# The third layer's entry and its second pass: first strips and bases on ScalarE's DMA queue, tables in pieces, later needs issued later, memory tracked by tiles

## The chip, the cores and the metric

The kernel runs on one core of a Trainium2 chip, in fp32. The metric is the device time of one execution in microseconds; the time of a kernel is the median of its runs.

## The reference, cut to what matters

The kernel applies four residual layers to an image batch `x` of shape (8, 56, 56, 192), each to the group-normalized `x` (32 groups of channels):

```
x = x + L0(gn(x))     # gated Toeplitz (decaying FFT convolution) along both axes
x = x + L1(gn(x))     # outlook attention, 3x3 neighbourhoods
x = x + L2(gn(x))     # gated attention in 8x8 windows, with a linear part over all windows
x = x + L3(gn(x))     # scans along rows, columns and diagonals
```

The change concerns the third layer, L2, cut here:

```
uvb = silu(xw @ W_uv + b_uv)                # xw: windows of 64 tokens, 192 channels
u, v, base = uvb[:384], uvb[384:768], uvb[768:]          # base: 128 wide
qq, qk = rope in the window of (base * gq_g + gq_b), (base * gk_g + gk_b)
lq, lk = rope in the image of (base * lq_g + lq_b), (base * lk_g + lk_b)
attn = square(relu(qq @ qk.T / 64 + rel_bias[REL_INDEX]))
kv   = sum over all windows of an image of lk.T @ v      # 128 x 384
out  = u * (attn @ v + lq @ kv) @ W_proj + b_proj
```

`kv` is needed as a whole before any output, so the layer makes two passes over the image.

## The kernel before, in words

The layers run one after the other in one program and keep x in DRAM between them. Images are worked on in pairs (`NPAIR` is 4): 128 of an image's 192 channels lie on the partitions of one tile, and the other 64 of both images share a second tile. In layer 1 and in the second pass of the third layer the instruction order on TensorE, VectorE (DVE), ScalarE (ACT) and GpSimd (POOL) is the order in which the source writes it (`manual_schedule`); in the first pass of the third layer that holds for TensorE alone, and the other engines' order, like that of the DMAs on SyncE (SP), is set by a planner when the program is built. Every engine then works through its queue in order, and a DMA is issued from the queue of the engine that the source names. A DMA or an instruction waits until the tiles that it writes are free and those that it reads are filled; between pools that follow each other in the same memory this is tracked by pool or, with `reuse_waits="tile"`, by tile.

**Group norms.** `GroupNormPairs` (L1135 on) holds a matrix `gmat` (576 KB) that spreads group sums over channels by tiny matmuls (L1153). The statistics of a pair are gathered strip by strip with `bn_stats` (L1007 in layer 1). At a pair's end three steps follow: `means`, `deviations` and `tell`. `deviations` and `tell` each use one burst of matmuls, `tell` also a square root on ACT (L1182) and four small DMAs that write the scales and shifts to DRAM as `norm`. In layer 1 these steps are put off into the next units as a list `late`; what remains in the list after the last unit is run at once, at the layer's end.

**Third layer, entry.** `layer2` (L1236) builds its own `GroupNormPairs` and the `Takeover` (L1194), which loads what the fourth layer needs (`am`, `vec`, `res`). Then SP fetches the norms of all four pairs (16 DMAs, L1262 and L1263). ACT's queue issues the weights of pass 2 (`wub`, `bub`, `wpr`, `bpr`, `gbs`) and four rotation tables, of which `cos_img` and `sin_img` have 1568 KB each. SP loads `ident`, the weights and bias of pass 1 (`wvb`, `bvb`) and the cos rows; ACT's queue loads the sin rows (1600 KB each). From these DVE and POOL make the key tables `tn`, `ta` and `tb`, 128 x 3200 each, in five operations (L1355 to L1359). Then the first two strips of x are fetched (`load`, L1276 to L1278: six DMAs per strip), the first is normalized (`wa`, `wb`, L1301, or L49 for the part that DVE takes), and SP issues 64 DMAs that lay out the relative bias row by row (L1466).

**Third layer, pass 1.** `groups` lists for each pair 13 groups of up to two chunks of 128 tokens of both images, 52 in all. In loop step n, group n is projected to v and base (`project`, PE `v` L1390), biased on DVE (`sm`, L1400) and passed through silu on ACT (`vb`, L1401); v is stored to DRAM (L1412) and base is turned into keys with the tables (`keys`: POOL L1419, L1420, DVE L1424, L1427). For group n-2, base is transposed and stored (`turn`, PE `t` L1436, ACT `bt` L1440) and the keys are summed with v (`sum_up`, PE `kv` L1450). `vb` has four buffers, the PSUM tile `v` three, the PSUM tile `t` one. A strip covers seven chunks, so a pair has four strips; `fetch` runs two strips ahead.

**Third layer, pass 2.** `units` lists strips of 448 tokens, 28 in all. `fetch2` issues the loads of a unit: x, the base both straight (`bt`, L1509) and with its halves swapped (`bs`, L1512), and v (`vt`, L1515). `rotate` makes qq, qk and lq from them (ACT L1524 and L1525, POOL L1535, DVE L1538 and L1539). TensorE starts a unit with the window products (`b`, L1550).

## Time and profile before

| what | value |
|---|---|
| three runs | 4262.56, 4271.02, 4275.62 us; median 4271.02 |
| profiled execution | 4265.11 us, of which its span is 4263.3 |
| granted TensorE clock, mean | 0.971 |
| TensorE busy | 3954.9 us, 93% of the span |
| VectorE, ScalarE, GpSimd busy | 55%, 42%, 35% |
| layer 1's last y matmul (L978) ends | 2724.2 us from the span's start |
| first projection of the third layer (L1390) | 2775.45 us |
| kv sums of groups 0, 1 and 2 (L1450) | 2812.13, 2820.80, 2829.36 us |
| last kv sum ends | 3225.08 us |
| first window product of pass 2 (L1550) | 3244.86 us |

The profile is one execution; its instants count from the start of its span. "Waited for" is idle time of an engine in front of an instruction, put down to what came last. Figures of one stage are read from windows of the trace, not from the shares of the whole span.

### The profile page before, as it was taken

How to read it: one execution, taken by the hardware profiler on the slowest of the kernel's cores; microseconds unless marked ns; L12 is line 12 of the kernel's file. 1: busy time of each engine (PE TensorE's matmuls, PEld its weight loads, DVE VectorE, ACT ScalarE, POOL GpSimd, SP SyncE). 2: the span in 40 equal slices, each digit the busy share in tenths (PEclk: the TensorE clock that was granted, in tenths of full speed). 3: DMA queues.
4: the chain of work that ended last, by engine and by line, in shares of the span. 5: the costliest groups of instructions: out<-in, count | busy, mean ns of one | idle time of the engine just before them, and what ended most of it. 6: DMA issues, size and time to landing. Idle time of an engine off the chain costs nothing.

```text
span 4263.3 us, 106441 instructions
## 1 busy us (share of the span) xinstructions
PE 3954.9 (93%) x46380; PEld 2553.1 (60%) x46380; DVE 2345.1 (55%) x3396; ACT 1781.1 (42%) x2020; POOL 1512.6 (35%) x1294
## 2 busy tenths in 40 slices
PE   6989999999999999999699999679998999998997
PEld 3666656666665656666366666434444555555997
DVE  4536565554656555464534444266666666664664
ACT  2434444334444433443233334133334555554664
POOL 3222232223223221332233333143334444444776
PEclk9999999999999999999799999889999999999999
DMA  6755242332524233241324444555547676664243
GB/s 142 141 106 145 62 114 71 81 86 62 145 62 115 74 81 84 62 122 47 92 75 107 97 105 108 146 153 169 166 141 186 167 166 162 151 156 112 73 115 94
DMA packets 379606, 484.13 MB, mean 114 GB/s; under 512 B 175780, under 2 KB 324372, under 8 KB 377236
## 3 DMA queue, kind: packets, MB, share of 16 engines
q1 hardware_dynamic: 373636, 466.97, 43.0%
q10 hardware_dynamic: 5504, 10.35, 0.8%
q8 instruction: 365, 5.98, 0.6%
q14 instruction: 101, 0.83, 0.1%
HBM read 321.49 MB, written 155.65 MB: 112 GB/s over the span
## 4 chain that ended last, share of the span: by engine, by line
PE 73%; DVE 7%; issue 7%; DMA 4%; SPq 3%; POOL 3%; ACT 2%; DVEq 0%; POOLq 0%; ACTq 0%
PE c L294 9%; PE v L1390 6%; PE c L395 6%; PE h L1892 5%; PE c L301 5%; PE c L481 4%; PE c L436 4%; PE c L943 4%; PE c L461 3%; PE y L978 3%; PE kv L1450 3%; PE c L443 3%; PE c L486 2%; DVE ol L357 2%; PE c L949 2%
## 5 line engine op out<-in xcount | busy, mean ns | idle before, releaser
L325 POOL TENSOR_TENSOR qv<-s,s 128x392 f32<-128x392 f32 (+3 forms) x320 | 569.3, 1799 | 1424.6 <-ACT s L310 1354.2
L294 PE MATMUL c<-xa,wqv 128*128 128x392 f32 x1152 | 435.9, 520 | 7.7 <-ACT or L357 4.8
L310 ACT ACTIVATE s<-c,bqv 128x784 f32<-128x784 f32 (+1 forms) x320 | 278.2, 910 | 389.9 <-PE c L301 232.8
L319 DVE TENSOR_TENSOR qv<-s,s 128x784 f32<-128x784 f32 (+1 forms) x160 | 190.4, 1190 | 268.2 <-ACT s L310 268.1
L357 ACT COPY or<-c 56x1024 f32<-56x1024 f32 x224 | 225.6, 1007 | 256.3 <-DVE ol L357 240.9
L294 PEld LDWEIGHTS c<-xa,wqv 128*128 128x128 f32 x1152 | 212.2, 196 | 177.2 <-issue 44.2
L395 PEld LDWEIGHTS c<-or,ol 120*64 120x64 f32 x9216 | 277.8, 138 | 55.7 <-issue 47.4
L395 PE MATMUL c<-or,ol 120*64 120x56 f32 x9216 | 287.2, 223 | 18.5 <-DMA ol<-ed 9.0
L357 DVE COPY ol<-c 56x1024 f32<-56x1024 f32 x224 | 261.4, 1208 | 63.4 <-PE c L352 63.4
L450 ACT ACTIVATE s<-c,bp 128x448 f32<-128x448 f32 x224 | 129.7, 630 | 271.0 <-PE c L443 271.0
L1390 PE MATMUL v<-wvb,wa 128*128 128x512 f32 (+1 forms) x400 | 192.6, 614 | 50.0 <-ACT wa L1301 30.7
L301 PE MATMUL c<-xb,wqv 64*128 64x392 f32 x1152 | 233.6, 519 | 0.0
L1923 POOL TENSOR_TENSOR y<-y,s 128x448 f32<-128x448 f32 x168 | 185.1, 1102 | 90.1 <-ACT s L1902 90.1
L1892 PE MATMUL h<-ringv,am 128*64 128x57 f32 (+1 forms) x4400 | 191.8, 235 | 18.3 <-DVE ringv L1879 11.3
L481 PE MATMUL c<-po,wo 128*128 128x448 f32 x448 | 198.1, 564 | 10.8 <-DVE po L470 10.8
L436 PE MATMUL c<-xa,wp 128*128 128x224 f32 x896 | 192.0, 358 | 3.2 <-issue 3.2
L1892 PE MATMUL h<-ringh,am 128*64 128x57 f32 (+1 forms) x4400 | 185.9, 231 | 8.0 <-DVE ringh L1898 7.8
L1401 ACT ACTIVATE vb<-sm 128x1024 f32<-128x1024 f32 (+1 forms) x100 | 103.7, 1038 | 211.2 <-issue 187.2
L424 DVE TENSOR_TENSOR acca<-c,acca 128x392 f32<-128x392 f32 (+1 forms) x120 | 67.3, 586 | 222.0 <-PE c L486 204.8
L352 PE MATMUL c<-ident,qv 64*120 64x64 f32 x3584 | 144.3, 227 | 44.2 <-ACT or L357 38.3
L1892 PEld LDWEIGHTS h<-ringv,am 128*64 128x64 f32 x4400 | 167.2, 140 | 21.5 <-DVE ringv L1879 12.2
L943 PE MATMUL c<-wv,xc 128*126 128x192 f32 x896 | 175.4, 339 | 0.7 <-DVE s L903 0.6
(224 smaller groups left out, 7690.6 us busy)
## 6 DMA issues: line engine op xcount, KB each, us to landing
or<-tt SPq DMA_DIRECT2D x252, 196.0 KB
ol<-tt SPq DMA_DIRECT2D x252, 196.0 KB
vt<-v SPq DMA_DIRECT2D x56, 672.0 KB
v<-vb SPq DMA_DIRECT2D x96, 384.0 KB
x<-x SPq DMA_DIRECT2D x112, 168.0 KB
x<-x SPq DMA_DIRECT2D x112, 112.0 KB
bt<-bs SPq DMA_DIRECT2D x28, 448.0 KB
bs<-bs SPq DMA_DIRECT2D x56, 224.0 KB
```

Of the source, the lines that this page charges most:

```text
L294: nc.tensor.matmul(ps[:, h, 0:n], wqv[0][:, j, :], xn[0][:, at : at + n], start=True, stop=False,)
L301: nc.tensor.matmul(ps[:, h, 0:n], wqv[1][rows, j, :], xn[1][rows, g * n : (g + 1) * n], start=False, stop=True,)
L310: nc.scalar.activation(t, ps[rows, :, 0:n], AF.Silu, bias=bqv[rows, j : j + 1])
L319: nc.vector.tensor_tensor(sub(qv[rows, 7 * g :, 64 + H - 1 :], (HH * 120, 2), (120, 7), (-1, H)), *(t.rearrange("p u (h w) -> p u h w", w= ...
L325: eng.tensor_tensor(sub(qv[rows, w0:, H - 1 - 7 * g - HH * u :], (120, w1 - w0), (-1, 7)), *(t[:, u].rearrange("p (h w) -> p w h", w=H)[:, ...
L357: copy(dst[:, :, :, i0 : i0 + 8], view[rows])
L395: nc.tensor.matmul(ps[u * 64 : (u + 1) * 64, k, v * H : (v + 1) * H], left[:, d * H : d * H + 64], right[:, d * H : (d + 1) * H], start=Tr ...
L436: nc.tensor.matmul(out(u, h), wp[0][:, 2 * j + u, :], xn[0][:, at : at + n], start=(u == 0), stop=True, skip_group_check=True,)
L481: nc.tensor.matmul(pa, wo[:, 2 * j + u, 0:CA], pos[u], start=(u == 0), stop=(u == 1))
L943: nc.tensor.matmul(out(i, u), group(i, u), wv[0], start=(u == 0), stop=True, skip_group_check=True,)
L1390: nc.tensor.matmul(out, x[:, at : at + n], wt, start=(k == 0), stop=(k == 1), skip_group_check=True,)
L1892: nc.tensor.matmul(ps[sides[c], y], am[a][:, m * CB : (m + 1) * CB], old[:, x], start=(n < 2), stop=True, skip_group_check=True,)
```

## The change

1. One `GroupNormPairs` is built before layer 1's pools and lives to the end of the program, on the other side of the memory (`side="right"`); the third layer uses it too. The statistics tile of layer 1 comes from its pool.
2. The steps left in layer 1's `late` list are not run at its end. They become jobs of pass 1's loop, at steps 3, 5 and 7, with their sums in the PSUM tile `t`.
3. The first strip, the norms of pair 0, `wvb`, `bvb` and `gk` are issued by ACT's queue. The second strip's loads stay on SP.
4. The key tables are loaded and made in pieces of six chunks (768 columns; the last has 128): the first ahead of the loop, the others at steps 1, 4, 7 and 10.
5. Jobs of the loop, on SP: the norms of pairs 1 to 3 at steps 9, 22 and 35; the weights of pass 2 at step 18; its tables at steps 20, 22, 24 and 26, the large ones in pieces of 448 columns; the bias eight rows at a time at steps 28 to 35 and its copy at 36; the `Takeover` loads at step 38.
6. The layer's pools track their memory by tiles.
7. In `fetch2`, `bs` and `bt` are issued before x and `vt`; for unit 0 by ACT's queue.

```diff
@@ layer1
+    cx.keep = ExitStack()
+    gn = cx.gn = GroupNormPairs(cx, cx.keep, w["gmat"])
...
-        gn = GroupNormPairs(cx, es, w["gmat"])
...
-                stats[p] = cx.tile(sp, [128, 3, NT, 6], "st", bufs=2)
+                stats[p] = cx.tile(gn.small, [128, 3, NT, 6], "st")
...
-        for _, f in late:
-            f()
+        cx.late = [f for _, f in late]
@@ layer2, entry
-        gn = cx.gn = GroupNormPairs(cx, cx.between, w["gmat"])
-        over = cx.over = Takeover(cx, consts)
-        cp = es.enter_context(tc.tile_pool(name="l2c", bufs=1))
+        gn, over = cx.gn, Takeover(cx)
+        cx.over = over
+        cp = es.enter_context(tc.tile_pool(name="l2c", bufs=1, reuse_waits="tile"))
...
+            gn.place = psk, "t"
+            raw, xws = {0: load(xp, 0, 0, 2, nc.scalar)}, {}
+            fetch_norms(0, nc.scalar)
+            wvb = [cx.tile(c1, [128, E + S], f"wvb{k}") for k in range(2)]
+            for k in range(2):
+                nc.scalar.dma_start(wvb[k], w[f"W_vb{k}"])
+            bvb = cx.tile(c1, [128, E + S], "bvb")
+            nc.scalar.dma_start(bvb, w["b_vb"].partition_broadcast(128))
             ident = cx.tile(c1, [128, 128], "ident")
             nc.sync.dma_start(ident, consts["ident"])
...
-            nc.sync.dma_start(ta, consts["cos_rows"])
-            nc.scalar.dma_start(tb, consts["sin_rows"])
-            nc.sync.dma_start(gk, w["lk_gb"].partition_broadcast(128))
...
-                nc.vector.tensor_tensor(tn, ta, g[2], ALU.mult)
-                nc.gpsimd.tensor_tensor(tmp, tb, g[3], ALU.mult)
-                nc.vector.tensor_tensor(ta, ta, g[0], ALU.mult)
-                nc.vector.tensor_tensor(tn, tn, tmp, ALU.add)
-                nc.gpsimd.tensor_tensor(tb, tb, g[1], ALU.mult)
...
+            def key_tables(c):
+                at = slice(c * TW, min((c + 1) * TW, NCH))
+                n = at.stop - at.start
+                a, b, t = ta[:, at], tb[:, at], tn[:, at]
+                nc.sync.dma_start(a, consts["cos_rows"][:, at])
+                nc.scalar.dma_start(b, consts["sin_rows"][:, at])
+                g = [gk[:, i, :].unsqueeze(1).to_broadcast([128, n, S]) for i in range(4)]
+                tmp = cx.tile(c1, [128, TW, S], "tmp")[:, 0:n]
+                nc.vector.tensor_tensor(t, a, g[2], ALU.mult)
+                nc.gpsimd.tensor_tensor(tmp, b, g[3], ALU.mult)
+                nc.vector.tensor_tensor(a, a, g[0], ALU.mult)
+                nc.gpsimd.tensor_tensor(b, b, g[1], ALU.mult)
+                nc.vector.tensor_tensor(t, t, tmp, ALU.add)
...
-            for n in range(2):
-                fetch(n)
             ready(0)
+            nc.scalar.dma_start(gk, w["lk_gb"].partition_broadcast(128))
+            key_tables(0)
+            fetch(1)
+            jobs = [(3 + 2 * k, f) for k, f in enumerate(cx.late)]
+            jobs += [(13 * p - 4, lambda p=p: fetch_norms(p)) for p in range(1, NPAIR)]
+            jobs += [(18, weights2), (38, lambda: over.load(consts))]
+            jobs += [(20 + 2 * k, lambda k=k: tables2(k)) for k in range(4)]
+            jobs += [(28 + k, lambda k=k: bias2(range(8 * k, 8 * k + 8))) for k in range(8)]
+            jobs += [(36, lambda: nc.sync.dma_start(bias[WT:], bias[0:WT]))]
             kept = {}
             for n in range(len(groups) + 2):
                 pvs = []
+                if n in (1, 4, 7, 10):
+                    key_tables((n + 2) // 3)
+                for at, job in jobs:
+                    if at == n:
+                        job()
@@ layer2, pass 2
...
+            bs = cx.tile(xp, [S, 2, SW], "bs")
+            queue = nc.sync if n else nc.scalar
+            for h in range(2):
+                queue.dma_start(bs[sides[h]], bst[p][sides[1 - h], :, cols])
+            bt = cx.tile(xp, [S, 2, SW], "bt")
+            queue.dma_start(bt, bst[p][:, :, cols])
             x = load(xp, p, r, 1)
```

`weights2`, `tables2`, `bias2` and `Takeover.load` hold the DMAs that stood at the entry before, now on SP.

## The prediction

> **What bounds the kernel now.** I read the page first, then windows of ten microseconds around the third layer's entry, then the waits and the chain there. On the page TensorE carries the kernel; a few of its forty slices are short, the 26th and 27th among them.
>
> ```profile
> PE 3954.9 (93%) x46380; PEld 2553.1 (60%) x46380; DVE 2345.1 (55%) x3396; ACT 1781.1 (42%) x2020; POOL 1512.6 (35%) x1294
> ...
> PE   6989999999999999999699999679998999998997
> ```
>
> Those two slices lie at 2664 to 2877 us. In the windows the columns are the window, then busy time (and instructions) of PE, its weight loads, DVE, ACT, POOL, then TensorE's clock, the DMA share and GB/s.
>
> ```profile
> 2740.00:2750.00 10.00, 3.83 (x18) 3.69 (x17) 0.98 (x6) 0.26 (x1) 0.00 (x0) 0.50 0.48 123
> 2750.00:2760.00 10.00, 0.00 (x0) 0.00 (x0) 0.17 (x1) 0.00 (x0) 0.30 (x1) 0.50 0.51 93
> 2760.00:2770.00 10.00, 0.00 (x0) 0.00 (x0) 0.00 (x0) 0.00 (x0) 0.00 (x0) 0.50 0.98 339
> 2770.00:2780.00 10.00, 2.08 (x2) 0.50 (x2) 7.63 (x2) 2.25 (x4) 7.44 (x1) 0.50 1.03 214
> 2780.00:2790.00 10.00, 0.00 (x0) 0.00 (x0) 10.00 (x2) 3.41 (x5) 9.92 (x2) 0.50 0.36 67
> 2790.00:2800.00 10.00, 3.20 (x4) 1.50 (x5) 8.69 (x5) 0.00 (x0) 2.75 (x1) 0.50 0.02 2
> 2800.00:2810.00 10.00, 10.00 (x30) 3.67 (x29) 4.95 (x4) 3.29 (x3) 2.54 (x2) 0.96 0.01 0
> ```
>
> From 2740 to 2800 TensorE works 9.1 us of 60, and that at clock 0.50. First data is missing, then VectorE and GpSimd are the busy ones. Who is waited for (engine, line, releaser: total, times, longest):
>
> ```profile
> PE v L1390 <- ACT wa L1301: 30.7, 1, 30.7
> ...
> ACT wa L1301 <- DMA xa<-x: 30.6, 2, 29.6
> ...
> PE v L1390 <- DVE wa L49: 19.3, 1, 19.3
> ```
>
> The first projection waits 30.7 us for a strip of x, whose loads (L1276 to L1278) SyncE issues only after the last norms have made three DMA trips (4.47, 2.98 and 2.98 us in the chain); the second waits 19.3 us for `wa`. Its maker, the affine of L49, takes 2.67 us for four, but stands in VectorE's queue behind the key tables:
>
> ```profile
> L1358 DVE TENSOR_TENSOR tn<-tn,tmp 128x3200 f32<-128x3200 f32 x1 | 10.2, 10204 | 0.0
> L1357 DVE TENSOR_TENSOR ta<-ta,gk 128x3200 f32<-128x3200 f32 x1 | 10.1, 10107 | 0.0
> L1356 POOL TENSOR_TENSOR tmp<-tb,gk 128x3200 f32<-128x3200 f32 x1 | 10.1, 10058 | 16.9 <-DMA xa<-x 16.9
> ```
>
> The chain (start, length, what) also runs along SyncE's 64 bias loads, from 2778.43 to 2823.7 us, behind which strip 2's loads and the stores of v stand:
>
> ```profile
> 2762.42 13.52 DMA xb<-x
> 2775.96 8.54 DMA xa<-x
> 2784.52 0.62 SPq L1466
> ...
> 2823.07 2.71 DMA bias<-in_l_rel_bias
> ```
>
> From the third sum of keys and values on (`kv` L1450 of group 2, at 2829.36) pass 1 is TensorE-bound: a group every 8.57 us. So my yardstick is that instant. Layer 1's last y matmul ends at 2724.2: 105.2 us lie between. Between the passes there is a second hole:
>
> ```profile
> 3225.00:3235.00 10.00, 0.07 (x1) 0.00 (x0) 0.56 (x1) 0.00 (x0) 0.00 (x0) 0.62 0.78 203
> 3235.00:3245.00 10.00, 0.14 (x3) 0.17 (x5) 7.23 (x5) 6.72 (x7) 6.25 (x3) 0.50 1.09 228
> ```
>
> PE b L1550 starts at 3244.86 after 19.8 us of idling; the rotation before it (ACT rs L1524, 3235.34) waited 10.7 us for `bs`.
>
> **What the Trainium skill says.** "DMA: Bandwidth & Descriptors", Issuing engines are not separate DMA queues: an added issuing queue saves only the sequencer's issue time, the same 16 engines move the data. The trace agrees on the price: SyncE's issues take 0.3 to 0.62 us each, and here 64 of them, 45 us, do matter. "GPSIMD Engine Reference", 1. Specifications: its SBUF interfaces are shared with VectorE, contended when VectorE has two SBUF inputs. The trace agrees in part: L1357 and L1358 beside POOL take 10.1 us, L1355 of the same shape 3.49 us. "TensorE: Matmul & The Clock Gate", Part 1, puts the clock at half after an idle window of 3.4 us; here it is 0.50 through the hole and 0.96 in the window from 2800. "ScalarE: Activation LUTs", What ACT_TABLE_LOAD costs: 1283 ns; the trace has 1283 ns (L1401).
>
> **The change, part by part.**
>
> (a) The strip no longer waits for the norms of the last pair, nor for anything issued after it. Its six loads go out by ACT behind `ys copy`, which ends at 2725.71: six times 0.5 us, 2725.8 to 2729. Pair 0's norm DMAs (4), wvb (2), bvb, gk and the tb pieces follow in that queue. In the built streams the norm loads wait for stores of the last unit, which before start about 2733 to 2736. With 3 us of landing norm 0 is there at about 2740.5. ACT then makes two `wa` (0.75 each) and one `wb`: first projection about **2742**, 33 us earlier than 2775.45. Queued behind these DMAs on ACT is only `wa` itself.
>
> (b) From PE's second release (2796.80) to `kv` of group 2 took 32.6 us. With 2.1 us more for the two matmuls that were then already done, 2742 gives 2776.7: 52 us gained if TensorE alone ruled. That is the best end.
>
> (c) The tables come in pieces of 768 columns. A piece is three DVE and two POOL instructions: at L1357's rate 10.1 x 768/3200 = 2.4 us, at L1355's 0.84 us. The first piece is 3.0 to 7.3 us of DVE ahead of the first `sm` (L1400). Its cos rows are on SyncE and land about 2743, so `sm` begins at about 2752.5 at the slow rate. Following the queues on from there with sm 1.22, vb 1.06, POOL l 1.45 and 1.32, DVE l 1.04 twice and 0.69, and with the second piece at loop step 1 and the third at step 4, `kv` stands at 2769, 2782 and 2791 for groups 0, 1, 2. Gain 38 us. In the steady state a third of a piece per group adds 2.4 us to DVE's some 5 of 8.57, and 1.6 to POOL's 2.8: hidden. I take **41 us**, nearer the slow end, since the trace shows that rate three times in four.
>
> (d) The last norm steps move into loop steps 3, 5 and 7. Two bursts of 14 tiny matmuls (L1153) took 3.13 us each in the hole at half clock; at full clock, inside layer 1, the chain has 1.65 us for such a burst. On a bound TensorE that is +3.3 us. Each uses the PSUM tile "t" of the transposes, so the next transpose waits for a DVE copy or ACT's sqrt: 1 to 3 us together, I take 2; a gain is excluded, since nothing starts earlier by it. ACT reloads its table for the sqrt and back, 2 x 1.28 us, beside 42% busy: nothing, unless `vb` is then late by it. Sum **+5.3 us**.
>
> (e) SyncE receives within pass 1 what stood at the entry: 64 bias issues as eight per group at steps 28 to 35 (8 x 0.7 = 5.7 us, 45.3/64 each), weights (7), tables (16 pieces), am, vec, res (5), norms (4 per pair). Its other work per group is two v stores, one bs store and on average 1.85 strip loads (24 for 13 groups), 4.85 x 0.6 = 2.9 us. The sum, 8.6 us, fills the period of 8.57. The cover is that strips are fetched about 30 us ahead and `vb` has four buffers; I cost it at nothing; its bounds are 0 and the last rival's loss. The bytes are those of before.
>
> (f) Pass 2: bs and bt of unit 0 go by ACT, which is free from the last `vb` on, at about 3224.9 where SyncE issued them at 3228.25 to 3229.5. `rs` starts 4.4 to 7 us earlier. The x loads then lie behind nothing new, unit 1's bs moves ahead of its x, vt lands later by two issues (1.3 us) and is needed only after attention. I take **5 us**. Bounds: 2 us lost if ACT's own queue, with `wa` and `rs` in it, is held by these issues or the transfers (DMA share 1.09) crowd bs; 8 gained if unit 1's 2.5 us wait goes too.
>
> (g) Waits by tile, memory on the other side, one gmat (576 KB) and one eps memset fewer: no instruction on the path. Layers 0, 1 and 3 keep their order of instructions in the built streams, so nothing there: between -4 and +4 us, as another placement could do.
>
> Sum: 41 - 5.3 + 5 = 40.7 us. The profiled execution took 4265.11 us (span 4263.3, 1.8 around it) and lies 5.9 us under the median of 4271.02; 4265.1 - 40.7 = 4224.4, beside the median 4230.3. I forecast **4229 us**.
>
> **Rivals.**
>
> *TensorE alone rules (0.22).* If pieces run at L1355's rate, DVE is out of the way by 2747: 52 - 5.3 + 7 = 54 us, 4217. For it: the hole has little else on POOL. Against: L1357 and L1358.
>
> *The first strip is late (0.15).* The 12 last x stores, the norm loads and 3 MB of ta and tb share the 16 DMA engines (share 0.86 to 0.99 from 2727 to 2742), and queues recycle completion semaphores. Strip 0 before took 13.5 us for one xb. Twelve microseconds later start leaves 41 - 12 - 5 + 3 = 27 us, or with 20 later, 19: 4244 to 4252.
>
> *The change doesn't do what it says (0.05).* If a wait by tile still ties the first strip to the stores of the last unit's statistics, or pieces to the whole table, only bias and pass 2 gain: some 5 to 12 us, 4259 to 4266.
>
> *SyncE becomes the bound (0.08), slower.* It is in order: a store that waits for `vb` holds the next strip and the bias rows behind it. The reserve is 30 us and the gain 41, so it must fall 71 us behind over steps 18 to 38, 3.6 us per group: it decides from about 12 us of SyncE per group. At 14 us, (14 - 8.57) x 20 - 71 = 38 us slower, 4309. For it: no slack in steps 28 to 35, and 2.71 us landing of a bias row. Against: eight DMAs in flight cover landing, and the entry issued 64 rows at 0.7 us.
>
> *The slow piece rate rules (0.50)* is my forecast.
>
> **How the numbers follow.** Faster by over 0.3% (12.8 us, about what a measurement can tell) takes the forecast, the first two rivals: 0.87 less some of the late strip, 0.86. Same is most of the third: 0.06. Slower: 0.08. The range begins at the best case with (g) and 4 us of scatter in its favour (4217 - 8 = 4209; the three times before spread over 13 us) and ends at 4262, beyond the late strip and half-way through the no-change case, which leaves out 2 in 10 with the slower one and the doubts of the steps.
>
> **What would show it.** Right: `v` L1390's successor waits under 20 us in all and starts near 2742; `kv` of group 2 at 2785 to 2792; no 64-row block in the chain; the hole between passes near 14 us; group pitch 8.57 us throughout, with two spots of about 1.7 us for gmat. Wrong: first `wa` later than 2750 (late strip), DVE or POOL waits on pieces after step 10, or PE waiting for `wa` or `vb` at steps 20 to 36 behind SyncE.

## The result, and the profile after

The changed kernel takes **4242.81 us**, median of four runs (4233.79 to 4244.47), beside 4272.33 us for the kernel before in the same measurement: ratio **0.993, 95% interval 0.9909 to 0.9952**, some 30 us faster (21 to 39). The forecast was 4229 us, 14 us less than came; the direction and the range (4209 to 4262) held. The profiled execution of after took 4244.47 us, its span is 4242.7, so that it lies 1.7 us above its median, where that of before lay 5.9 under: the two profiles differ by 20.6 us, the medians by 29.5.

First the page of after, the same two lines as of before (busy time by engine, then TensorE in forty slices):

```profile
PE 3956.6 (93%) x46380; PEld 2552.2 (60%) x46380; DVE 2340.2 (55%) x3407; ACT 1785.8 (42%) x2022; POOL 1510.7 (36%) x1302
...
PE   6999999999999999999689999889998999998997
```

The busy times are those of before to within 5 us. What moved is idle time: the 26th and 27th slice, the entry, show 8 and 8 where before had 6 and 7. The page says no more than that, so I went to the windows (window, then busy time and instructions of PE, its weight loads, DVE, ACT, POOL, then TensorE's clock, DMA share, GB/s):

```profile
2740.00:2750.00 10.00, 0.00 (x0) 0.00 (x0) 4.67 (x11) 2.19 (x4) 0.00 (x0) 0.51 0.84 245
2750.00:2760.00 10.00, 8.95 (x17) 3.51 (x18) 0.78 (x1) 3.25 (x5) 0.00 (x0) 0.64 1.01 280
2760.00:2770.00 10.00, 3.08 (x6) 1.22 (x5) 5.54 (x7) 2.34 (x2) 5.38 (x3) 0.70 1.03 248
2770.00:2780.00 10.00, 7.55 (x19) 2.62 (x17) 9.43 (x6) 1.06 (x1) 9.84 (x5) 0.79 0.49 153
2780.00:2790.00 10.00, 6.63 (x12) 3.28 (x12) 10.00 (x9) 2.59 (x3) 5.29 (x4) 0.66 0.24 87
```

From 2750 to 2770 the DMA engines are full (share 1.01 and 1.03) and POOL begins only at 2764.54; from 2770 to 2780 DVE and POOL are full (9.43 and 9.84 us of ten) and TensorE waits for them. The waits of that stage (who, for whom: total, times, longest) name both limits:

```profile
ACT wa L1306 <- DMA norm<-norm: 17.5, 1, 17.5
...
PE v L1417 <- DMA wvb<-in_l_W_vb: 15.1, 1, 15.1
DVE tn L1387 <- DMA gk<-in_l_lk_gb: 9.8, 1, 9.8
...
PE v L1417 <- DVE sm L1427: 6.9, 1, 6.9
...
PE kv L1477 <- DVE l L1454: 6.7, 2, 5.8
```

Instants below are counted from the end of layer 1's last y matmul ("y end", 2724.17 before, 2728.74 after). That is needed: over the fourteen profiles of this study y end scatters from 2715.5 to 2733.1, also among kernels with the same layers 0 and 1, so the 4.6 us between these two profiles can't be put down to the change. The account of the two profiles, with what the forecast's steps said:

| stage | before | after | difference | forecast |
|---|---|---|---|---|
| layers 0 and 1, to y end | 2724.2 | 2728.7 | +4.6 | 0 |
| y end to `kv` of group 2 (a, b, c) | 105.2 | 75.2 | -30.0 | -41 |
| on to the last `kv` (d, e) | 395.7 | 396.7 | +1.0 | +5.3 |
| hole between the passes (f) | 19.8 | 15.1 | -4.7 | -5 |
| pass 2 | 664.3 | 665.4 | +1.1 | 0 |
| entry of the fourth layer (g) | 8.0 | 12.9 | +5.0 | 0 |
| rest of the fourth layer | 346.2 | 348.6 | +2.4 | 0 |

So eleven microseconds are missing at the entry, and five are lost at the fourth layer's entry, where the forecast put nothing.

**Why the entry gained 30 and not 41.** The timeline of after, ACT's queue, DVE and POOL together (start, length, engine, line, what, and the idle time before it with its releaser):

```profile
2743.10 0.34 ACTq L1267 DMA_DIRECT2D norm<-norm  x1
...
2746.46 0.82 ACTq L1365 DMA_DIRECT2D wvb<-in_l_W_vb  x2
...
2750.76 0.33 ACTq L1484 DMA_DIRECT2D gk<-in_l_lk_gb  x1
...
2754.39 0.33 ACTq L1384 DMA_DIRECT2D tb<-in_sin_rows  x1
2754.78 1.41 ACT L1306 ACTIVATE wa<-xa,norm 128x448 f32<-128x448 f32 x2 [4.25 <-DMA ta<-in_cos_rows]
...
2764.54 1.80 POOL L1388 TENSOR_TENSOR tmp<-tb,gk 128x768 f32<-128x768 f32 x1 [33.65 <-DMA xb<-x]
2766.38 0.96 DVE L1391 TENSOR_TENSOR tn<-tn,tmp 128x768 f32<-128x768 f32 x1 [4.46 <-POOL tmp L1388]
2767.25 1.22 DVE L1427 TENSOR_TENSOR sm<-v,bvb 128x1024 f32<-128x1024 f32 x1
...
2772.40 5.04 DVE L1387 TENSOR_TENSOR tn<-ta,gk 128x768 f32<-128x768 f32 x2
2777.36 3.42 DVE L1451 TENSOR_TENSOR l<-vb,tb 128x256 f32<-128x256 f32 x2
```

Read it from the top. The strip's own loads had gone by 2734.5, but the norm loads behind them stood on ACT's queue until 2743.10, while SyncE issued the last twelve x stores of layer 1 (2734.36 to 2743.94); `wvb` stood behind the norms, and TensorE waited for `wvb`. `gk` went out behind `wvb` and the strip's first four normalizing steps. The first sin rows stood until 2754.39. The `wa` behind them on ACT shows this wait: it ended when cos rows landed, which `wa` doesn't read. These were the rows of the second piece, issued by SyncE at 2748.13, for the planner had put the cos rows of four pieces together (2745.83 to 2749.43). In this program the DMAs of both queues share eight completion semaphores (a counter that tells of a landing; in after SP used each of them 348 to 353 times, ACT 3 to 8 times), and in the trace an issue waits until the DMA that used its semaphore before has landed. So rows of later pieces held those of the first, and POOL could begin the first piece only at 2764.54.

Then two steps of later pieces, 5.04 us at 2772.40, run ahead of the first key step (L1451), for which TensorE's `kv` waits 5.81 us. The first `sm` came 38.5 us after y end, where the forecast had 28.3.

### The profile page after: what moved, and what is told of

It reads as the page before. It is cut to its first block, busy times and chain, and to the rows that moved or that the text cites. A ratio compares the mean times of both kernels' runs of the same rounds, so it can differ in the third digit from the quotient of the medians.

```text
span 4242.7 us, 106499 instructions
## 1 busy us (share of the span) xinstructions
PE 3956.6 (93%) x46380; PEld 2552.2 (60%) x46380; DVE 2340.2 (55%) x3407; ACT 1785.8 (42%) x2022; POOL 1510.7 (36%) x1302
## 5 line engine op out<-in xcount | busy, mean ns | idle before, releaser
L1925 PE MATMUL h<-ringv,am 128*64 128x57 f32 (+1 forms) x4400 | 192.1, 235 | 24.7 <-DVE ringv L1912 17.7
L1417 PE MATMUL v<-wvb,wa 128*128 128x512 f32 (+1 forms) x400 | 194.5, 619 | 22.0 <-DMA wvb<-in_l_W_vb 15.1
```

What stands on the lines that cost most here:

```text
L1417: nc.tensor.matmul(out, x[:, at : at + n], wt, start=(k == 0), stop=(k == 1), skip_group_check=True,)
L1925: nc.tensor.matmul(ps[sides[c], y], am[a][:, m * CB : (m + 1) * CB], old[:, x], start=(n < 2), stop=True, skip_group_check=True,)
```

## The experiments

All are edits of after unless said otherwise. The table has the main instants after y end, the entry of the fourth layer (last matmul of pass 2 to first `h`), and the ratio to the kernel before on the same chip.

| kernel | first v | kv 2 | kv 20 | fourth layer's entry | ratio, 95% interval |
|---|---|---|---|---|---|
| before | 51.3 | 105.2 | 257.2 | 8.0 | 1 |
| after | 22.3 | 75.2 | 228.2 | 12.9 | 0.9930, 0.9909 to 0.9952 |
| e1 pass 2 alone | 53.2 | 106.8 | 258.1 | 12.9 | 0.9998, 0.9988 to 1.0008 |
| e2 tile order | 22.6 | 76.8 | 229.8 | 7.9 | 0.9919, 0.9899 to 0.9939 |
| e3 whole tables | 25.3 | 79.6 | 237.5 | 13.0 | 0.9959, 0.9943 to 0.9975 |
| e4 gk first | 26.7 | 74.9 | 229.9 | 12.9 | 0.9939, 0.9917 to 0.9960 |
| e5 no products | 21.7 | 57.8 | 212.4 | 13.0 | 0.9903, 0.9887 to 0.9918 |
| e6 pinned | 22.4 | 60.8 | 226.8 | 12.9 | 0.9939, 0.9924 to 0.9953 |
| e7 norm steps at the end | 34.2 | 81.9 | 231.7 | 12.9 | 0.9947, 0.9933 to 0.9960 |
| e8 combined | 15.0 | 56.8 | 223.4 | 7.9 | 0.9914, 0.9898 to 0.9929 |
| e9 loads ahead | 17.1 | 59.7 | 227.5 | 7.9 | 0.9907, 0.9890 to 0.9923 |
| e10 first loads by SyncE | 25.3 | 66.3 | 225.7 | 12.9 | 0.9908, 0.9885 to 0.9931 |
| e11 bias in a block | 23.0 | 58.5 | 229.2 | 13.0 | 0.9931, 0.9911 to 0.9952 |
| e12 steps later | 14.7 | 57.0 | 213.9 | 7.9 | 0.9885, 0.9868 to 0.9902 |

In every row kv 20 is read at the fifth of that group's eight matmuls, 1.3 us after its first; the differences between rows don't depend on it. From there to the last `kv` every one of them takes 243.8 us, 8.57 per full group: from kv 20 on pass 1 is TensorE's alone.

**e1: the kernel before with the new order of pass 2's loads alone.**

```diff
+            bs = cx.tile(xp, [S, 2, SW], "bs")
+            queue = nc.sync if n else nc.scalar
...
+            bt = cx.tile(xp, [S, 2, SW], "bt")
+            queue.dma_start(bt, bst[p][:, :, cols])
             x = load(xp, p, r, 1)
```

> The kernel before with the change's part in fetch2 alone (bs and bt created and issued before x and vt, unit 0's by ScalarE's queue). Theory: this part brings 4.7 us in the hole between the passes (19.8 to about 15 us of idle TensorE), and takes 5 us at the fourth layer's entry (from the last pyb matmul's end to the first h: 8.0 to about 13 us), because the order in which tiles are created shifts them, so that u0 of the fourth layer lies over x tiles whose last stores are still to finish. Total within 3 us of before. Rival: the fourth layer's 5 us come from another part (Takeover loads, placement of the group norm's tiles): then the hole shrinks, the entry stays at 8.0 and the total falls by some 5 us.

Measured 4267.99 us beside 4269.24. The hole shrinks from 19.8 to 15.7 us, the fourth layer's entry grows from 8.0 to 12.9. The two cancel: this part of the change is worth nothing as it stands.

**e2: after, tiles created in the old order, loads issued in the new one.**

```diff
+            x = cx.tile(xp, [CA, 2, SW], "xa"), cx.tile(xp, [128, SW], "xb")
+            vt = cx.tile(xp, [128, 7, E], "vt")
+            bt = cx.tile(xp, [S, 2, SW], "bt")
             bs = cx.tile(xp, [S, 2, SW], "bs")
...
-            bt = cx.tile(xp, [S, 2, SW], "bt")
             queue.dma_start(bt, bst[p][:, :, cols])
-            x = load(xp, p, r, 1)
-            vt = cx.tile(xp, [128, 7, E], "vt")
+            load(xp, p, r, 1, x=x)
```

> The changed kernel with fetch2's tiles created in the old order (xa, xb, vt, bt, bs) and the DMAs issued in the new one. Theory: the fourth layer's entry goes from 12.9 back to 8.0 us with the hole between the passes still near 15 us; total 5 us under the changed kernel, ratio to before near 0.992. Rival (the 5 us have nothing to do with where x lies): the entry stays near 12.9 us and the total is that of the changed kernel.

Measured 4235.28 us, entry of the fourth layer 7.9 us, the hole still 16.0. The three timelines show why. Before, the fourth layer's first ACT step starts with no wait:

```profile
3909.74 5.88 ACT L1841 ACTIVATE u<-y,co 128x3136 f32<-128x3136 f32 x2
```

In after it waits for the last stores of x, which SyncE issues until 3884.81:

```profile
3884.36 0.45 SPq L1656 DMA_DIRECT2D x<-xb  x1
...
3886.78 5.90 ACT L1874 ACTIVATE u<-y,co 128x3136 f32<-128x3136 f32 x2 [4.94 <-DMA x<-xb]
```

and with e2's order of creation the wait is gone:

```profile
3873.44 5.88 ACT L1876 ACTIVATE u<-y,co 128x3136 f32<-128x3136 f32 x2
```

So the order in which the tiles are created costs the 5 us, and the order of the loads was not at fault. The reading that fits the wait is that tiles lie in memory in the order of their creation: with `bs` and `bt` created ahead of x, the x tiles of the last units came to lie where the fourth layer's `u` is put, and `u` had to wait until they were stored. The traces do not show the addresses.

**e3: the whole tables at once, before the loop.**

```diff
-            TW = 6
+            TW = NCH
```

> The changed kernel with the key tables loaded and made in one piece (TW = all 25 chunks) ahead of the loop. Theory (the first sm waits for the first sin piece to land and for its DVE steps): landing of 1600 KB each and three operations of up to 10 us put the third kv sum 20 to 28 us later than in the changed kernel, so nearly all of the entry's 30 us is the pieces' doing. Rival (the strip's path rules, the pieces are a side matter): the third kv sum is less than 8 us later.

Measured 4251.45 us. At kv 2 it is only 4.4 us later than after, at kv 20 9.2 later: my theory of 20 to 28 us fell, and cutting the tables is a side matter of the entry. Its timeline, POOL and DVE, is the clearest on why:

```profile
2764.71 6.92 POOL L1388 TENSOR_TENSOR tmp<-tb,gk 128x3200 f32<-128x3200 f32 x1 [36.65 <-PE v L1417]
2771.66 3.49 DVE L1391 TENSOR_TENSOR tn<-tn,tmp 128x3200 f32<-128x3200 f32 x1 [8.14 <-POOL tmp L1388]
2771.71 10.26 POOL L1390 TENSOR_TENSOR tb<-tb,gk 128x3200 f32<-128x3200 f32 x1
2775.07 2.35 DVE L1427 TENSOR_TENSOR sm<-v,bvb 128x1024 f32<-128x1024 f32 x2
```

POOL takes 6.92 us when DVE stands. Beside a DVE step of 3.49 us that started 0.05 us earlier, the same work takes 10.26, very nearly 3.49 and 6.92 one after the other. The Trainium skill ("SBUF — State Buffer", Who interferes with whom) has the rule: a DVE instruction with two SBUF inputs contends with a GpSimd instruction that reads SBUF, for ports that are an exclusive lock, and the order of issue decides who is blocked. The trace agrees, and so does that of before, where the five steps take turns:

```profile
2772.34 3.49 DVE L1355 TENSOR_TENSOR tn<-ta,gk 128x3200 f32<-128x3200 f32 x1 [13.22 <-DMA gk<-in_l_lk_gb]
2772.56 10.06 POOL L1356 TENSOR_TENSOR tmp<-tb,gk 128x3200 f32<-128x3200 f32 x1 [16.87 <-DMA xa<-x]
2775.86 10.11 DVE L1357 TENSOR_TENSOR ta<-ta,gk 128x3200 f32<-128x3200 f32 x1
2782.70 10.05 POOL L1359 TENSOR_TENSOR tb<-tb,gk 128x3200 f32<-128x3200 f32 x1
2785.89 10.20 DVE L1358 TENSOR_TENSOR tn<-tn,tmp 128x3200 f32<-128x3200 f32 x1
```

Each one that comes second ends about 6.8 (POOL) or 3.3 us (DVE) after the other engine's step has ended, and the row takes 23.8 us where 3 x 3.49 + 2 x 6.92 is 24.3. `sm`, whose first input is in PSUM, is not held: 1.2 us each as ever. So the 10.1 us that the forecast took for a slow rate were a queue for one port, 3.5 us of work and 6.6 of waiting.

**e4: `gk` issued ahead of the norm loads on ACT's queue.**

```diff
             nc.scalar.dma_start(bvb, w["b_vb"].partition_broadcast(128))
+            gk = cx.tile(c1, [128, 4, S], "gk")
+            nc.scalar.dma_start(gk, w["lk_gb"].partition_broadcast(128))
+            fetch_norms(0, nc.scalar)
```

> The changed kernel with wvb, bvb and gk issued on ScalarE's queue ahead of pair 0's norms, gk no longer behind the normalization of strip 0. Theory (order of issue made gk and the first sin piece land late, 2759 and 2764 us, and the table steps themselves are quick): gk and the sin piece land 5 to 8 us earlier, norms 2 us later; first sm 5 to 8 us and third kv sum 4 to 8 us earlier, first projection up to 3 us later. Rival A (the DMA engines are full, share 1.0, so order only exchanges waits): third kv sum within 2 us of the changed kernel. Rival B (the prediction's: contended DVE and POOL rates set it): the table steps take 7 us for the first piece wherever they start, third kv sum within 3 us.

Measured 4240.5 us, kv 2 unchanged (74.9, after 75.2), as both rivals had it. POOL's first step came at 2753.81, 28.2 us after y end in place of 35.8, yet the first `sm` still stood at 40.4. DVE's timeline shows what had the time:

```profile
2755.90 0.96 DVE L1392 TENSOR_TENSOR tn<-tn,tmp 128x768 f32<-128x768 f32 x1 [0.41 <-POOL tmp L1389]
2756.78 2.57 DVE L1390 TENSOR_TENSOR ta<-ta,gk 128x768 f32<-128x768 f32 x1
2759.27 5.03 DVE L1388 TENSOR_TENSOR tn<-ta,gk 128x768 f32<-128x768 f32 x2
2764.22 1.81 DVE L1390 TENSOR_TENSOR ta<-ta,gk 128x768 f32<-128x768 f32 x2
2765.95 1.21 DVE L1428 TENSOR_TENSOR sm<-v,bvb 128x1024 f32<-128x1024 f32 x1
```

The first piece is finished at 2756.9; then come five steps of pieces 1 to 3, which nobody needs yet, and then `sm`, which TensorE waits for. Only TensorE's order is written by hand in this pass. It looks as if the planner fills DVE with whatever has its inputs early; the run shows the order and not the planner's reason.

**e5: the tables' products left out.**

```diff
-                nc.vector.tensor_tensor(t, a, g[2], ALU.mult)
-                nc.gpsimd.tensor_tensor(tmp, b, g[3], ALU.mult)
...
+                nc.vector.tensor_tensor(t[:, :, 0:2], a[:, :, 0:2], g[2][:, :, 0:2], ALU.mult)
```

> The changed kernel without the products of the key tables (four of the five operations of each piece are left out, the fifth is cut to two columns per chunk; keys are made from the raw tables, so their values differ). From the end of layer 1's last y matmul the changed kernel has its first projection at +22.3, first sm at +38.5, third kv sum at +75.2 us. Theory (the landing of gk and the first sin piece, and the table steps standing ahead of sm and of the key steps on VectorE, cost the entry some 10 us): first sm at +31 to +33, third kv sum 8 to 14 us earlier. Rival (the transfers of strips rule, tables are beside it): third kv sum less than 4 us earlier. The products' cost in the steady state is nil in both.

Measured 4224.77 us; kv 2 at 57.8, 17.4 us earlier, more than I had expected. From the first projection to kv 2 it takes 36.1 us (57.8 - 21.7), after 52.9. So the products and their place in the queues are 17 us of the entry, the larger cause, and this is the bound to measure a better order against: kv 20 at 212.4.

**e6: later pieces kept at their place in the program.**

```diff
+                keep = tc.keep_in_program_order if c else lambda ins: ins
+                keep(nc.sync.dma_start(a, consts["cos_rows"][:, at]))
+                keep(nc.scalar.dma_start(b, consts["sin_rows"][:, at]))
...
+                keep(nc.vector.tensor_tensor(t, a, g[2], ALU.mult))
+                keep(nc.gpsimd.tensor_tensor(tmp, b, g[3], ALU.mult))
```

> The changed kernel with the loads and the first two operations of table pieces 1 to 4 kept behind what the source has ahead of them on their engines, so that they can't be issued before sm of group 0. Theory (planned too early, the pieces hold both the DMA engines, 2.3 MB, and VectorE): gk and the first sin piece land some us earlier, the key steps of group 0 no longer stand behind five table steps, third kv sum 6 to 14 us earlier. Rival (a piece issued later is late for its groups): the gain at the third kv sum is given back at the sixth or ninth, as a TensorE wait for the l of group 3 or 6.

Measured 4241.19 us. kv 2 comes at 60.8, 14.4 us earlier and close to e5's. Of these 14.4, 3.9 are there by the first `sm` (34.6, after 38.5) and 10.5 come after it. The pins hold back the later pieces' loads and their products, and this run doesn't tell the two apart. But 13.0 us are given back between kv 2 and kv 20 (166.0 us, after 153.0). The rival had the mechanism: the later pieces' rows are now loaded when they are needed, and layer 1's norm steps meet DVE while it catches up. TensorE's waits:

```profile
PE t L1464 <- DVE gms L1175: 5.6, 1, 5.6
```

`gms` is the copy of the norms' sums out of the PSUM tile `t`, which the next transpose needs.

**e7: the norm steps run at layer 1's end again.**

```diff
-        cx.late = [f for _, f in late]
+        for _, f in late:
+            f()
+        cx.late = []
```

> The changed kernel with the last group-norm steps run at layer 1's end again, as before. Prediction's step d had them cost 5.3 us inside pass 1 (3.3 of matmuls and 2 of handing over the tile t). Theory: pass 1 from the third to the last kv sum loses the 3.4 us of two bursts and no more (396.7 to 393.3), for the handover shows no wait; the entry is 0 to 5 us later, for ScalarE's square root stands ahead of pair 0's norm loads and waits for the sums. Total within 4 us of the changed kernel. Rival (the steps kept the entry waiting by their DMAs): entry later by 10 us or more.

Measured 4243.63 us. Pass 1 from kv 2 on is 3.1 us shorter (393.6, after 396.7), the first projection 11.9 us and kv 2 6.6 us later. In the hole each burst of 14 matmuls takes 3.12 us and waits for DVE; in after, inside pass 1, 1.72 us:

```profile
2735.78 3.12 PE L1155 MATMUL b<-mean,gmat 128*128 128x1 f32 x14 [6.22 <-DVE mean L1172]
2739.84 3.12 PE L1155 MATMUL b<-dev,gmat 128*128 128x1 f32 x14 [0.93 <-DVE dev L1179]
```

Moving them pays, 3.5 us by these stages; the ratio alone (0.9947 beside 0.993, intervals that overlap) could not say so.

**e8: the cures together.** e2's order of tiles, e6's pins, `gk` early, pair 0's norms in memory that nothing in layer 1 uses, issued before the strip, and the pools of pass 1 stacked in another order.

```diff
-            n = norms[p] = cx.tile(cp, [128, 3, 2], f"norm{p}")
+            n = norms[p] = cx.tile(gn.pool, [128, 3, 2], f"norm{p}")
...
+            wk = pool("l2w1", 2)
             c1 = pool("l2c1", 1)
             xp = pool("l2x1", 2)
-            wk = pool("l2w1", 2)
...
-            raw, xws = {0: load(xp, 0, 0, 2, nc.scalar)}, {}
             fetch_norms(0, nc.scalar)
+            raw, xws = {0: load(xp, 0, 0, 2, nc.scalar)}, {}
```

> A version meant to beat both: the changed kernel with fetch2's tiles created in the old order; table pieces 1 to 4 kept behind earlier work as in the pinned run; gk issued with wvb and bvb; pair 0's norms in the memory of the group norm and issued first; and the pass-1 pools stacked as work, constants, strips, so that the early loads lie over memory that is freed early. Theory (the entry's rest is memory that frees late, issue order and tables planned too early): first projection at +16 to +19 from layer 1's last y matmul, third kv sum at +57 to +64 instead of +75.2; fourth layer's entry 8 instead of 12.9; total 16 to 23 us under the changed kernel, about 4223. Rival (the DMA engines' throughput bounds the entry whatever the order): third kv sum not under +70, total only 5 to 9 us under the changed kernel.

Measured 4230.82 us. `wvb` goes out 11.4 us after y end (after: 17.7), the first projection starts at 15.0. The norm loads themselves now went out at 2395.7 to 2417.1, over 300 us before y end. That agrees with one reading of after's timeline: the norm loads had to wait until layer 1 was done with the memory that they write. Another is open, for in after the waits of three of the four end at the landing of an x store (issued 2740.79 to 2743.02) whose semaphore they take over. e8 moved them both in memory and in the queue, and doesn't tell these apart. kv 2 stands at 56.8. Then 13.6 us are given back up to kv 20, as in e6. That part of my expectation missed, and with it the total: some 7 us under after by the ratios, where 16 to 23 were expected.

**e9: e8 with the rows of each piece loaded one to two steps ahead of its products.**

```diff
+                if n in (0, 2, 5, 8):
+                    key_tables((n + 1) // 3 + 1, make=False)
                 if n in (1, 4, 7, 10):
-                    key_tables((n + 2) // 3)
+                    key_tables((n + 2) // 3, load=False)
```

> The combined version with the loads of table pieces 1 to 4 issued at loop steps 0, 2, 5 and 8 and made at 1, 4, 7 and 10 as before (in e8_combined both came at one step, and VectorE stood 2.8, 2.3 and 7.5 us before pieces 2, 3 and 4). Theory: third kv sum at +57 to +61 from layer 1's last y matmul as in e8_combined, and from the third to the eleventh kv sum 71 to 75 us instead of 84.5; total 8 to 13 us under e8_combined's stages, 20 us under the changed kernel, ratio to before near 0.988. Rival (the pieces' steps on VectorE, not their loads, hold up sm): the 84.5 stay above 80.

Measured 4223.09 us. From kv 2 to kv 10 it takes 78.2 us (e8: 84.5, after: 70.9): loads ahead help by half, where 71 to 75 were expected. But kv 2 comes 2.9 us later than in e8, and kv 20 even 4.1; the ratios of the two, 0.9907 and 0.9914, don't differ beyond their intervals. What is left is in two places. A transpose waits 4.2 us for `gms` as in e6, and later POOL stands for a load of the fourth layer:

```profile
2920.71 0.31 POOL L1216 TENSOR_SCALAR vec<-vec,res 128x3 f32<-128x3 f32 x1 [15.24 <-DMA res<-in_l_res]
2920.98 1.26 POOL L1452 TENSOR_TENSOR l<-vb,ta 128x512 f32<-128x512 f32 x1
...
2924.36 5.13 PE L1483 MATMUL kv<-vb,l 128*128 128x384 f32 x8 [5.04 <-DVE l L1460]
```

A step of 0.31 us that nothing needs for a thousand microseconds was planned ahead of a key step and waited 15.24 us for its data, which SyncE issued only at 2915.6.

**e10: the first loads by SyncE's queue.**

```diff
-            raw, xws = {0: load(xp, 0, 0, 2, nc.scalar)}, {}
-            fetch_norms(0, nc.scalar)
+            raw, xws = {0: load(xp, 0, 0, 2)}, {}
+            fetch_norms(0)
...
-                nc.scalar.dma_start(wvb[k], w[f"W_vb{k}"])
+                nc.sync.dma_start(wvb[k], w[f"W_vb{k}"])
```

with `bvb` and `gk` likewise.

> The changed kernel with the first strip, pair 0's norms, wvb, bvb and gk issued by SyncE instead of ScalarE's queue (unit 0 of pass 2 stays as changed). Theory (what helps is that the strip no longer stands behind the last norms and 16 norm loads; the queue itself saves only the time that SyncE spends on layer 1's 12 last stores, 2734 to 2744): first projection 3 to 10 us later than +22.3, third kv sum 0 to 8 us later than +75.2. Rival (the own queue is what brings the entry's gain): third kv sum 15 us or more later.

Measured 4225.84 us, 0.9908. The first projection is 3.0 us later, kv 2 8.9 us **earlier**, with 6.3 given back to kv 20. Both theories missed the sign. In its timeline the first piece's three DVE steps are followed at once by the first two `sm` (39.4 us after y end) and the first key step (44.0; after: 48.6), as the second piece comes later (its cos rows go out 44.9 us after y end; after: 19.4). So ACT's own queue isn't what carries the gain.

**e11: the 64 bias rows at step 0, in a block, as before.**

```diff
-            jobs += [(28 + k, lambda k=k: bias2(range(8 * k, 8 * k + 8))) for k in range(8)]
+            jobs += [(0, lambda k=k: bias2(range(8 * k, 8 * k + 8))) for k in range(8)]
```

> The changed kernel with all 64 bias rows issued in one block at loop step 0 instead of eight per step at 28 to 35 (the copy stays at step 36). Theory (prediction's step e: SyncE's issue time is hidden as long as strips are fetched ahead and vb has four buffers): 45 us of SyncE delay strip 2 and v's stores, costing TensorE 0 to 6 us once before the sixth kv sum, total within 6 us of the changed kernel. Rival (the block was a bound of the entry, as the chain of before shows it): 10 to 30 us later, as a wait of vb for its stores or of wa for strip 2.

Measured 4234.71 us, 0.9931: as after. The block ran on SyncE from 2745.96 to 2788.97. It kept the later pieces' cos rows from being loaded, so that DVE did the keys first (kv 2 at 58.5, 16.7 us earlier), and then it held the next strip of x, issued behind it from 2789.07 on. ACT stood for that strip, `bt` stood behind on ACT's queue, and then 3.88 us more for a `bs` store that had been held by the block too; TensorE waited for `bt`, and from kv 2 to kv 5 it took 17.7 us longer. The total is the one expected, but as the sum of two larger moves, and the loss is of the size and kind that the rival named. Of its timeline, ACT and TensorE:

```profile
2793.28 1.41 ACT L1306 ACTIVATE wa<-xa,norm 128x448 f32<-128x448 f32 x2 [15.23 <-DMA xa<-x]
...
2803.58 3.15 PE L1154 MATMUL t<-mean,gmat 128*128 128x1 f32 x14 [12.75 <-ACT bt L1467]
```

**e12: e9 with the norm steps at 13, 15 and 17, and POOL's `vec` step at 46.**

```diff
-            jobs = [(3 + 2 * k, f) for k, f in enumerate(cx.late)]
+            jobs = [(13 + 2 * k, f) for k, f in enumerate(cx.late)]
...
+            jobs += [(18, weights2), (38, lambda: over.load(consts)), (46, over.add)]
```

> The version with loads ahead of the pieces, and two further moves: the last norm steps of layer 1 come at loop steps 13, 15 and 17 in place of 3, 5 and 7, when the tables are done; and GpSimd's addition to vec is pinned to loop step 46, eight steps after its load is issued, in place of wherever the planner put it. Theory (TensorE's remaining stalls in pass 1 are these two steps, the 4.2 us wait of a transpose for the norm's sums and the 5.0 us wait behind the 15.2 us that GpSimd stood for res): kv of group 2 about 58 to 61 us after layer 1's last y matmul as before this move, kv 2 to kv 20 153 to 158 us in place of 167.9, hole 15, entry of the fourth layer 8 us; in all 8 to 12 us less than the version with loads ahead by the sum of these stages, some 20 us under the changed kernel, ratio to the kernel before about 0.986 to 0.988. Rival (the planner, which lays out VectorE's and GpSimd's order anew after any such move, puts other late work ahead of a key step): kv 2 to kv 20 stays over 162 us with waits on other instructions, total within 4 us of the version with loads ahead, ratio 0.990 or more.

Measured **4219.77 us** (4213.36 to 4222.85) beside 4268.51: 0.9885. kv 2 stands at 57.0, and from kv 2 to kv 20 it takes 157.0 us, within the 153 to 158 expected. At kv 20 it stands 1.5 us behind e5, in which the products were not made at all. TensorE's waits from layer 1's end to kv 20, all of them:

```profile
PE v L1428 <- DVE sm L1438: 8.9, 3, 5.5
PE v L1428 <- ACT wa L1312: 7.5, 1, 7.5
PE c L1022 <- POOL ys L990: 2.2, 1, 2.2
PE kv L1488 <- DVE l L1465: 1.4, 1, 1.4
```

It has the lowest ratio of all, though its interval overlaps those of e5, e9 and e10. Against after, 0.9885 beside 0.993 is some 19 us; the intervals don't meet. The stages say 14.3 at kv 20 and 5.0 at the fourth layer's entry.

## Why the prediction was right, and where it fell short

Right in direction and range. Of its steps, (b) and (f) held, (a), (d) and (g) were off in size, and (c) and (e) stood on an order of instructions that didn't come; that these two did no more harm is in part luck. 16 of the 41 us that it summed are missing in the stages that the change touches (-25 in the table, without layers 0 and 1).

- **(a)**, the first projection 17.8 us after y end: it came at 22.3. The failed term is "With 3 us of landing norm 0 is there at about 2740.5". The wait for the stores of layer 1 was seen, but not how long these take to go out (until 2743.94; before, from 2729.79 to 2741.34), nor that `wvb` behind them on the same queue would come last. In e8, with the norms in memory of their own and first on the queue, it came at 15.0. The term is 4.5 us.
- **(b)**, the best end of 52 us: nearly confirmed. It has 34.7 us from the first projection to kv 2; e5, without products, took 36.1.
- **(c)**, 38 us at the slow rate, 41 taken: 30.0 came, 6.5 us of the lack beyond (a). The rate was misread: DVE and POOL exclude each other (e3), and the first piece's DVE steps, with POOL standing, ran at 0.91 to 0.96 us. Two steps failed. One is "Its cos rows are on SyncE and land about 2743": the piece also needs `gk` and the sin rows from ACT's queue, and its first DVE step waited for `gk` until 30.5 us after y end, where the forecast had the piece start at 18.8. In after the first `sm` is 10.2 us late by this. With `gk` early (e4) the piece started at 23.8 and `sm` came no earlier, for then the other failed step had it wait. That one is "Following the queues on from there ... with the second piece at loop step 1 and the third at step 4": it took the order of the source for the order on DVE, though the front part of this text says that a planner sets it. Steps of pieces 1 to 3 ran ahead of the first `sm` and the first keys (e4), and with pins kv 2 came 14.4 us earlier (e6). In e12 the second piece's rows go out as early as in after (19.4 us after y end in both) with the products pinned, and kv 2 still comes at 57.0: that speaks for the order of the products more than that of the loads, though e12 differs from after in more than this. From the first `sm` to kv 2 the forecast had 38.5 us (2791 less 2752.5) and 36.7 came; I read that as two errors against each other, and not as the rate confirmed. (Two slips of the working change nothing: three times 0.84 is 2.5 us and not 3.0, and four of the five table steps, not three of four, had the slow rate.)
- **(d)**, +5.3: e7 shows 3.1, the bursts alone (forecast 3.3). The handover of `t`, taken as 2, cost nothing in after. It is real where DVE is loaded at that step: 5.6 us in e6, 4.2 in e9.
- **(e)**, nothing: the cost is right, the way to it was not tried. The forecast weighed eight bias rows per group at steps 28 to 35, which filled SyncE's period to 8.6 of 8.57 us; its seven loads of weights are six. Those eight are the steps of the source. In after the planner issued the 64 rows from 2820.89 to 2903.1, at loop steps 6 to 16 by TensorE's place at the time, and the weights of pass 2, of step 18, from 2776.41:

```profile
2776.41 0.90 SPq L1322 DMA_DIRECT2D wub<-in_l_W_u  x2
...
2820.89 4.93 SPq L1343 DMA_DIRECT2D bias<-in_l_rel_bias  x7
...
2900.19 2.88 SPq L1343 DMA_DIRECT2D bias<-in_l_rel_bias  x4
```

  TensorE waited 0.6 us in all from kv 2 to the end of the pass. e11 adds that spreading the bias brought nothing either: as a block at the entry it held back table pieces that were in the way, and cost as much afterwards.
- **(f)**, 5 us: 4.7 in the hole, and 4.1 alone in e1.
- **(g)**, "no instruction on the path": wrong by 5.0 us. The step "Layers 0, 1 and 3 keep their order of instructions in the built streams, so nothing there" has the fourth layer in it (layer 3, counted from 0), and allowed 4 us either way for another placement. e1 and e2 show that tiles created in another order in the layer before are enough for a wait there.

Of the **rivals**, "TensorE alone rules" fell (6.9 us for `sm` and 6.7 for `l`, in TensorE's waits). "The first strip is late" asked for 12 us or more and got 4.5; its time is near the one measured, its mechanism a smaller part of it. SyncE as the bound didn't come, nor did the crowding at steps 28 to 35 that it rests on. "Doesn't do what it says" fell with the first projection 29 us earlier. Of the signs given, the pitch of 8.57 and the bursts of about 1.7 us came as said, the waits of `v`, under 20 us by the forecast, were 22.0, the hole near 14 came as 15.1, and kv 2 at 2785 to 2792 came at 2804, 2799.4 with y end as before.

What stays open: that e10's keys came forward because its second piece came later is read from its timeline, not tested, and so is the part that the shared semaphores have in the late start. In pass 1 the planner also lays out four engines' order anew after every edit (e10 and e11 moved kv 2 by 9 and 17 us without an edit to the tables), so that no edit there acts alone. Open too is how much of the 2.4 us in the rest of the fourth layer is the change, as that stage scatters by 10 us over the fourteen profiles with no edit in it.

## What to carry to other kernels

Where a planner orders an engine, moving an instruction in the source doesn't say when it runs, and it may run far ahead of its place: read the order on the engine that the next stage waits for, and pin the late work, with its loads ahead of it. Before a load is put at the head of a queue, ask when the memory that it writes comes free and which DMA had its semaphore before, since everything behind it on that queue waits too. An order of creation of tiles is an order in memory: to change when loads are issued, leave the creation where it was, and look at the entry of the next layer.

## What the runs showed of the hardware that I had not expected

DVE and POOL on SBUF operands did not slow each other, they took turns: 3.49 and 6.92 us became 10.26 for the second (e3), and 0.96 and 1.80 us on 768 columns became about 2.5 for each in a row of such pairs. A piece therefore costs the sum of its five operations, 3 x 0.96 + 2 x 1.80 = 6.5 us of one port, whichever engine has them. All five on DVE would take 5 x 0.96 = 4.8 us by the same figures, an estimate that no run tests.

The DMAs of two queues were tied by eight shared semaphores: in after the first sin rows stood on ACT's queue until 2754.39, when cos rows of another piece, issued by SyncE, had landed.

And two layers whose instructions no experiment edited up to y end ended anywhere within 17.6 us from profile to profile. Stages of a few microseconds could be told apart only from an instant within the same profile.
